# First attention of an eight-layer kernel: the mixture's largest weights loaded in sixteen pieces, and the next sequence's normalization moved half a pair of heads forward

## The chip, the cores and the metric

The kernel runs on one core of a Trainium2 chip. A core has TensorE (PE: matrix products; its weight loads, PEld, are shown apart), VectorE (DVE), ScalarE (ACT), GpSimd (POOL) and SyncE (SP), which only starts DMAs here. Each engine works through its own queue in order; semaphores let one engine wait for another or for a DMA. The metric is the device time of one launch in microseconds (us), as the median of several runs; less is better.

## The reference, cut to what matters

The reference is a chain of eight layers over `x` of 4 sequences x 1024 tokens x 128 channels: attention, mixture of experts, gated attention, the mixture again, a state space layer, a gated feed-forward layer, a second attention, and the feed-forward layer again. The change touches the first attention and the weights of the mixture:

```python
x = x + attention(layernorm(x))     # 16 heads of 64, causal
x = x + mixture(layernorm(x))       # 8 experts, 2 per token

def attention(x):                   # per sequence and head
    q, k, v = x @ Wq, x @ Wk, x @ Wv
    s = where(causal, -big, (q / 8) @ k.T)
    return softmax(s) @ v -> all heads @ Wo + bo

# mixture: W1 (8, 128, 512) and W2 (8, 512, 128), 2 MB each
h = relu(buf[e] @ W1[e] + b1[e]);  y = h @ W2[e] + b2[e]
```

## The kernel before, in words

The layers follow each other. `x` stays in SBUF throughout. The constructors of all layers load their weights first, on SP's queue, the first attention's own (Wq, Wk, Wv, Wo) on ACT's queue. Two loads are deferred: `load_late` (L91) puts the load of W1 and that of W2 (2 MB each, L496 and L497) as closures into a list `k.late`, ahead of which the state space layer has put a small exp on ACT (L1033, result `a`), with its DVE partner in `k.late_v` (L1034). The mixture needs W1 and W2 only after the first attention is over.

**First attention.** It works on 32 pairs of heads n, eight for each of the four sequences. For a pair, the queries are taken in four units (n, gq), gq = 0 to 3, of two blocks of 128 rows each; block i sees the first i + 1 blocks of keys. `first_stages` and `probabilities` make the scores (PE, L352), take them out of PSUM with the mask and the running minimum of their negatives (DVE, L358, a custom instruction that writes `p` and `tops`), and take the exponential with the sum (ACT, L367). At the end of a unit DVE forms the reciprocal `r` of the sums (L380), SP writes it to DRAM (`shares`, L383, 512 elements of 4 bytes) and reads it back spread over the partitions (`share`, L386). This first stage runs ahead of the second by up to 20 blocks of scores (`ahead`, `LEAD`).

`outputs` is the second stage: for each step PE transposes two columns of blocks of `p` into PSUM tiles `t` (L426), one is copied to `pt` by DVE (L433) and one by ACT (L431), and one step later PE multiplies `pt` with the values into `o` (L451). At the end of a unit DVE multiplies `o` by `share` into `ot` (L458). PSUM gives `s` two buffers, `t` two, `o` one, and the other products one (`ps_m`).

Between the steps one element of a list `pieces` is run at a time: projections of the pair after next (L280, L291), the output product of the pair before (`joined`, L318, L322), and, once in a sequence, the transposes of the normalized next sequence. `normalized(b)` (L248) computes the layer norm of sequence b into `xl`: eight statistics and eight aggregations on DVE (L117, L119), a square root on ACT (L121, which has to load another function table than the exponential and later load the old one back), a reciprocal (L122) and eight scalings (L124) on DVE; then POOL adds the bias `bo` to `x` (L251); then it appends two pieces that transpose `xl` to `xt` (L260). It is called ahead of unit (n, 0) when n + 2 is the first pair of a sequence, so for n = 6, 14 and 22.

**What sets the order.** `k.order()` gives chains (`pe`, `ve`) that keep PE's and part of DVE's instructions in the order in which the program writes them; the rest is placed by a scheduler, which also places the semaphore waits. DMAs started by hardware queues take turns on eight semaphore lanes: a DMA waits on its issuing engine until the DMA that had its lane before has landed.

The deferred loads are released in `probabilities`: at the first unit with gq = 2, after the exp of its first block (block 4), the whole list is run at once, pinned behind that exp in ACT's queue.

Of the kernel before, what the change touches and what calls it, by code (L numbers as in the profile page):

```python
# [21 lines left out]
B = 4  # L22
# [39 lines left out]
class Kernel:  # L62
# [28 lines left out]
    def load_late(self, pool, name, shape, src):  # L91

        t = pool.tile(shape, F32, name="w_" + name)
        self.late.append(lambda: self.nc.scalar.dma_start(t, src))
        return t

    def broadcast_row(self, pool, name, width):
# [97 lines left out]
class AttentionA:  # L195
# [11 lines left out]
    Q = 2  # L207
    NQ = NC // 2
# [12 lines left out]
    def __call__(self, start=None):  # L221
        k, tc, nc = self.k, self.k.tc, self.k.nc
        wq, wk, wv, wo, bo = self.wq, self.wk, self.wv, self.wo, self.bo
        Q, NQ, NP = self.Q, self.NQ, HEADS // 2
        scale = 1.0 / math.sqrt(DH_A)
        with self.stack as ctx:
# [15 lines left out]
                out=mask[:, MW - P :], in_=mask[:, MW - P :], compare_op=ALU.is_ge, fill=MASKED, base=0,  # L242
                pattern=[[-1, P]], channel_multiplier=1,
            )
            xts, pairs, units = {}, {}, {}
            pieces = []

            def normalized(b):  # L248
                xl = one.tile([P, NC, C], F32, tag="xl", name="xl")
                k.normalize(xl, k.xb(b), pin=ve)  # L250
                nc.gpsimd.tensor_tensor(  # L251
                    k.xb(b), k.xb(b), bo.unsqueeze(1).to_broadcast([P, NC, C]), ALU.add
                )

                def turned(h):
                    if h == 0:
                        xts[b] = one.tile([P, T], F32, tag="xt", name="xt")
                    ps = ps_m.tile([P, 512], F32, tag="m", name="ps")
                    for c in range(4):
                        pe(nc.tensor.transpose(ps[:, c * P : (c + 1) * P], xl[:, h * 4 + c, :], k.ident))  # L260
                    k.evacuate(xts[b][:, h * 512 : (h + 1) * 512], ps)

                pieces.extend([(NP * b, lambda: turned(0)), (NP * b, lambda: turned(1))])

            def projected(n):

                b, g = divmod(n, NP)
                cols = slice(g * P, (g + 1) * P)
                qt = sb.tile([P, T], F32, tag="qt", name="qt")
                kt = sb.tile([P, T], F32, tag="kt", name="kt")  # L270
                if g % 2 == 0:
                    both = sb.tile([P, NC, 2 * P], F32, tag="vv", name="vv")
                    for m in range(2):
                        pairs[n + m] = dict(v=both[:, :, m * P : (m + 1) * P])
                pairs[n].update(q=qt, k=kt)

                def features(to, w, h):
                    half = slice(h * 512, (h + 1) * 512)
                    ps = ps_m.tile([P, 512], F32, tag="m", name="ps")
                    pe(nc.tensor.matmul(ps, w[:, cols], xts[b][:, half], start=True, stop=True))  # L280
                    if w is wq:
                        nc.scalar.mul(to[:, half], ps, scale)
                    else:
                        nc.vector.tensor_copy(to[:, half], ps)

                def values(h):

                    ps = ps_m.tile([P, 2, 2 * P], F32, tag="m", name="ps")
                    for c in range(2):
                        j = h * 2 + c  # L290
                        pe(nc.tensor.matmul(  # L291
                            ps[:, c, :], xts[b][:, j * P : (j + 1) * P], wv[:, g * P : (g + 2) * P],
                            start=True, stop=True,
                        ))
                    k.evacuate(both[:, h * 2 : h * 2 + 2, :], ps)

                pieces.extend([
                    (n, lambda: features(qt, wq, 0)), (n, lambda: features(kt, wk, 0)),
                    (n, lambda: features(qt, wq, 1)), (n, lambda: features(kt, wk, 1)),
                ])  # L300
                if g % 2 == 0:
                    pieces.extend((None, lambda h=h: values(h)) for h in range(4))
# [33 lines left out]
            def probabilities(n, gq):  # L336

                q, kk = pairs[n]["q"], pairs[n]["k"]
                p = (late if gq == NQ - 1 else one).tile(
                    [P, 2, Q, (gq + 1) * Q * P], F32, tag=f"p{gq}", name="p"  # L340
                )
                tops = sb.tile([P, 2, Q, 2], F32, tag="tops", name="tops", bufs=3)
                sums = sb.tile([P, 2, Q], F32, tag="sums", name="sums")
                for i in range(Q):
                    ib = gq * Q + i
                    width = (ib + 1) * P
                    for at, lo in enumerate(range(0, width, 512)):
                        hi = min(lo + 512, width)
                        s = ps_s.tile([P, 2, 512], F32, tag="s", name="s")
                        for h in range(2):  # L350
                            feats = slice(h * DH_A, (h + 1) * DH_A)
                            pe(nc.tensor.matmul(  # L352
                                s[:, h, : hi - lo], q[feats, ib * P : (ib + 1) * P], kk[feats, lo:hi],
                                start=True, stop=True,
                            ))
                        m = mask[:, MW - hi + lo :] if hi == width else mask[:, : hi - lo]
                        for h in range(2):
                            ve(nc.vector.tensor_tensor_reduce(  # L358
                                p[:, h, i, lo:hi], s[:, h, : hi - lo], m, -1.0, 3.4e38, ALU.add, ALU.min,
                                tops[:, h, i, at : at + 1],  # L360
                            ))
                        if hi < width:
                            yield (hi - lo) // P
                    if width > 512:
                        nc.vector.tensor_tensor(tops[:, :, i, 0], tops[:, :, i, 0], tops[:, :, i, 1], ALU.min)  # L365
                    for h in range(2):
                        exp = nc.scalar.activation(  # L367
                            p[:, h, i, :width], p[:, h, i, :width], AF.Exp, bias=tops[:, h, i, 0:1],
                            scale=-1.0, accum_out=sums[:, h, i : i + 1],
                        )  # L370
                    if k.late and gq == 2:
                        pin = k.order()
                        pin(exp)
                        while k.late:
                            pin(k.late.pop(0)())
                        while k.late_v:
                            ve(k.late_v.pop(0)())
                    if i == Q - 1:
                        r = sb.tile([P, 2, Q], F32, tag="r", name="r")
                        nc.vector.reciprocal(r, sums)  # L380

                        there = dram.tile([2, Q, P], F32, tag="shares", name="shares")
                        nc.sync.dma_start(there.rearrange("h i p -> p h i"), r)  # L383
                        share = sb.tile([P, Q * P], F32, tag="share", name="share", bufs=4)
                        for h in range(2):
                            nc.sync.dma_start(  # L386
                                share[h * DH_A : (h + 1) * DH_A],
                                there[h : h + 1].rearrange("h i p -> h (i p)").to_broadcast([DH_A, Q * P]),
                            )
                        units[n, gq] = p, share  # L390
                    yield (hi - lo) // P

            def first_stages():
                for n in range(B * NP):
                    while n not in pairs or any(owner == n for owner, _ in pieces):
                        yield None
                    for gq in range(NQ):
                        yield from probabilities(n, gq)
# [48 lines left out]
            def product(n, gq, o, share, products, last, at_end):  # L447
# [7 lines left out]
                if at_end:  # L455
# [4 lines left out]
                    )  # L460

            normalized(0)
            projected(0)
            projected(1)
            ahead()
            for n in range(B * NP):
                for gq in range(NQ):
                    if gq == 0 and n + 2 < B * NP and (n + 2) % NP == 0:
                        normalized((n + 2) // NP)
                    if gq == 1 and n > 0:  # L470
                        joined(n - 1)
                    if gq == 3 and n + 2 < B * NP:
                        projected(n + 2)
                    outputs(n, gq)
# [1359 lines left out]
```

## Time and profile before

| | |
|---|---|
| median of 3 runs | 3373.56 us (3370.95 to 3374.28) |
| the profiled execution, its own time | 3378.53 us |
| its span, first to last instruction | 3376.7 us |
| mean granted clock of PE | 0.947 of full speed |
| first attention, from the first transpose to the last product into `ot` | 9.7 to 1220.6 us |
| bytes moved by DMAs, whole span | 109.35 MB |
| ACT's load of W1, issued | 34.8 us, 0.38 us long |
| ACT's load of W2, issued | 50.3 us, 0.88 us long |
| square root of the normalization, four times in the stage | 0.30 us each |
| scalings of the normalization (L124), 128x128 | 0.34 us each |
| last product into `ot` of pairs 0 to 6 ends at | 106.4, 142.8, 177.1, 213.5, 247.9, 290.0, 326.2 us |

A row of the profile names the line of the program, the engine, the operation and the tiles (written <- read). In the order of time a row has the start and the length in us; in brackets stands how long the engine was idle before it and what ended that. A row of windows has, for each engine, the busy time and the number of instructions in that stretch, then the clock that PE was granted, the mean busy share of the DMA engines, and GB/s. A duration of PE is to be read with the clock: at 0.5 the same product takes twice as long.

### The profile page before, as it was taken

The page shows a single profiled execution, that of the slowest core. Times are in us where ns is not written, and L with a number is a line of the kernel's source. Part 1 is how long each engine was busy: PE and PEld are TensorE (multiplying, and loading weights), DVE is VectorE, ACT ScalarE, POOL GpSimd, SP SyncE. Part 2 cuts the span into 40 slices and gives each one's busy share as a digit, 9 for nine tenths or more (in the row PEclk, how much of TensorE's full clock was granted, in tenths as well). Part 3 has the DMA queues.
Part 4 walks back from the last instruction along what each step waited for, and adds up shares of the span by engine and source line. Part 5 has one row for each costly group of instructions (what it writes and reads, how often), then busy time and mean ns, then how long its engine had stood idle before and what let it go on. Part 6 is the DMA issues. An engine that isn't in the chain of part 4 may idle for free.

```text
span 3376.7 us, 45533 instructions
## 1 busy us (share of the span) xinstructions
PE 3015.2 (89%) x16624; PEld 1655.0 (49%) x16624; DVE 2306.0 (68%) x5281; ACT 1812.9 (54%) x3819; POOL 273.0 (8%) x269
## 2 busy tenths in 40 slices
PE   5999999999999979869988597978778799999988
PEld 2555555555455547635566344444445344444435
DVE  3666666666776656666566589897977677677634
ACT  2555555555555523445423597979654265556662
POOL 1000000000000002530013200000001101010000
PEclk8999999999999989989999798989999699899999
DMA  5110111111110101100001111111111112121100
GB/s 156 16 16 14 15 18 16 14 17 17 14 17 15 15 8 32 53 10 1 0 16 40 53 64 50 57 57 51 63 38 42 34 44 53 31 51 31 30 2 25
DMA packets 149537, 109.35 MB, mean 32 GB/s; under 512 B 91760, under 2 KB 130432, under 8 KB 146880
## 3 DMA queue, kind: packets, MB, share of 16 engines
q1 hardware_dynamic: 128352, 72.84, 9.4%
q0 software_dynamic: 17408, 27.32, 3.3%
q10 hardware_dynamic: 3552, 6.29, 0.6%
q8 instruction: 130, 2.13, 0.4%
q14 instruction: 95, 0.78, 0.1%
HBM read 90.76 MB, written 15.60 MB: 31 GB/s over the span
## 4 chain that ended last, share of the span: by engine, by line
PE 68%; DVE 11%; ACT 8%; DMA 6%; issue 6%; POOL 1%; SPq 0%; DVEq 0%; ACTq 0%; POOLq 0%
PE s L352 8%; PE t L426 8%; PE o L451 8%; PE acc L649 4%; PE o L1613 4%; PE acc L1227 4%; PE x L1579 3%; PE ps L280 3%; PE acc L948 3%; PE s L1515 3%; ACT p L1585 3%; DMA shares<-r 2%; ACT hc L1226 2%; DVE st L1214 2%; DVE tops L1524 2%
## 5 line engine op out<-in xcount | busy, mean ns | idle before, releaser
L358 DVE CUSTOM_DVE_ANT_0 p<-s,mask 128x512 f32<-128x512 f32 (+3 forms) x768 | 394.6, 553 | 170.5 <-PE s L352 168.3
L367 ACT ACTIVATE p<-p,tops 128x640 f32<-128x640 f32 (+7 forms) x512 | 391.7, 767 | 146.1 <-DVE tops L365 85.4
L1585 ACT ACTIVATE p<-x 128x512 f32<-128x512 f32 (+3 forms) x768 | 337.6, 490 | 246.4 <-PE x L1584 176.6
L1524 DVE TENSOR_REDUCE tops<-s 128x2 f32<-128x1024 f32 (+3 forms) x384 | 361.3, 956 | 133.8 <-PE s L1520 94.2
L431 ACT COPY pt<-t 128x512 f32<-128x512 f32 (+1 forms) x320 | 157.7, 493 | 380.0 <-PE t L426 379.5
L1227 PE MATMUL acc<-hc,ident 128*128 128x512 f32 x512 | 270.1, 652 | 93.2 <-ACT hc L1226 92.3
L352 PE MATMUL s<-kt,qt 64*128 64x512 f32 (+3 forms) x1536 | 339.4, 533 | 2.7 <-DVE tops L358 2.6
L451 PE MATMUL o<-pt,vv 128*64 128x256 f32 (+1 forms) x2560 | 323.3, 374 | 14.7 <-ACT pt L431 9.4
L426 PE MATMUL t<-ident,p 128*128 128x128 f32 x2304 | 326.2, 282 | 3.7 <-DVE pt L433 3.0
L426 PEld LDWEIGHTS t<-ident,p 128*128 128x128 f32 x2304 | 248.1, 142 | 103.3 <-issue 70.0
L1214 DVE TENSOR_TENSOR_SCAN st<-decay,st 128x1024 f32<-128x1024 f32 x128 | 288.8, 2279 | 10.9 <-ACT decay L1211 10.4
L451 PEld LDWEIGHTS o<-pt,vv 128*64 128x64 f32 x2560 | 156.6, 137 | 263.9 <-issue 157.3
L433 DVE COPY pt<-t 128x512 f32<-128x512 f32 x320 | 220.0, 687 | 66.0 <-PE t L426 66.0
L1579 PE MATMUL x<-q,k 75*128 75x512 bf16 (+3 forms) x768 | 223.1, 338 | 27.7 <-ACT p L1585 15.0
L1515 PE MATMUL s<-k,q 72*128 72x512 bf16 (+3 forms) x768 | 216.3, 348 | 31.9 <-DVE tops L1524 17.6
L1226 ACT ACTIVATE hc<-ps,by_time 128x256 f32<-128x256 f32 x512 | 200.7, 478 | 50.6 <-PE ps L1220 50.5
L352 PEld LDWEIGHTS s<-kt,qt 64*128 64x128 f32 x1536 | 112.5, 188 | 180.7 <-issue 139.7
L1227 PEld LDWEIGHTS acc<-hc,ident 128*128 128x128 f32 x512 | 91.7, 198 | 209.6 <-ACT hc L1226 191.0
L738 POOL DMA_INDIRECT got<-y_rows,rows x128 | 136.7, 1068 | 645.1 <-DMA y_rows<-y 543.5
L1213 DVE TENSOR_TENSOR st<-du,bs 128x1024 f32<-128x1024 f32 x128 | 151.8, 1217 | 49.4 <-PE ps L1220 49.2
L649 PE MATMUL acc<-d,xl 128*128 128x480 f32 (+1 forms) x384 | 152.8, 559 | 26.2 <-DVE d L644 26.2
L1220 PEld LDWEIGHTS ps<-ident,st 128*128 128x128 f32 x1024 | 126.0, 146 | 96.5 <-issue 60.7
(272 smaller groups left out, 4740.7 us busy)
## 6 DMA issues: line engine op xcount, KB each, us to landing
bs<-b_rows SPq DMA_DIRECT2D x64, 512.0 KB
share<-shares SPq DMA_DIRECT2D x256, 64.0 KB
k<-b_parts POOLq DMA_DIRECT2D x16, 576.0 KB, 13.2
q<-b_parts POOLq DMA_DIRECT2D x48, 192.0 KB, 12.1
b_parts<-part SPq DMA_DIRECT2D x24, 256.0 KB
y_rows<-y SPq DMA_DIRECT2D x16, 192.0 KB
x<-in_x_dram SPq DMA_DIRECT2D x4, 512.0 KB
w_W<-in_W_dram ACTq DMA_DIRECT2D x1, 2048.0 KB
```

The lines of the kernel that those rows point to most:

```text
L352: pe(nc.tensor.matmul(s[:, h, : hi - lo], q[feats, ib * P : (ib + 1) * P], kk[feats, lo:hi], start=True, stop=True,))
L358: ve(nc.vector.tensor_tensor_reduce(p[:, h, i, lo:hi], s[:, h, : hi - lo], m, -1.0, 3.4e38, ALU.add, ALU.min, tops[:, h, i, at : at + 1],))
L367: exp = nc.scalar.activation(p[:, h, i, :width], p[:, h, i, :width], AF.Exp, bias=tops[:, h, i, 0:1], scale=-1.0, accum_out=sums[:, h, i : ...
L426: pe(nc.tensor.transpose(t[:, h, i * P : (i + 1) * P], p[:, h, i, jb * P : (jb + 1) * P], k.ident))
L451: pe(nc.tensor.matmul(o[feats, lo:], pairs[n]["v"][:, jb, feats], pt[:, h, lo:], start=jb == 0, stop=jb == last,))
L649: pe(nc.tensor.matmul(acc[n][:, :m, :].rearrange("p e s -> p (e s)"), xl[:, c, :], d[:, e : e + m, :].rearrange("p e s -> p (e s)"), start ...
L1214: nc.vector.tensor_tensor_scan(st, decay, st, 0.0, ALU.mult, ALU.add)
L1227: nc.tensor.matmul(acc[:, c : c + 2, :].rearrange("p c d -> p (c d)"), k.ident, hc.rearrange("p c d -> p (c d)"), start=n == 0, stop=n == ...
L1515: start.pin(nc.tensor.matmul(s[:, a, : hi - lo], qq[:ROWS, two + a, ib * P : (ib + 1) * P], kk[:ROWS, two + a, lo:hi], start=True, stop=ha ...
L1524: nc.vector.tensor_reduce(tops[:, half, two : two + 2, n], s[:, :, : hi - lo], AX.X, ALU.max)
L1579: start.pin(nc.tensor.matmul(x[:, lo:], kk[:FULL, a, jb * P : (jb + 1) * P], qq[:FULL, a, hq * 512 + lo : (hq + 1) * 512], start=True, sto ...
L1585: nc.scalar.activation(p[:, a, lo:], x[:, lo:], AF.Exp)
```

## The change

Two edits. The deferred loads become sixteen DMAs of 256 KB, one per expert and matrix; one element of the list is run at the end of a unit (after the exps of its second block), from unit (0, 2) on, so the small exp `a` in (0, 2) and the pieces in (0, 3) to (4, 2). And `normalized(b)` is cut in two: its arithmetic (DVE, ACT, POOL) runs ahead of unit (n, 2) with n + 3 the first pair of a sequence (n = 5, 13, 21); the rest, now `across(b)`, which only appends the two pieces of transposes, stays ahead of unit (n, 0) with n + 2 the first pair (n = 6, 14, 22). The scheduler leaves PE's order as it was. Around the third place it also moves statistics of the mixture's first two normalizations, and sets four table loads there in place of two.

```diff
@@ load_late
         t = pool.tile(shape, F32, name="w_" + name)
-        self.late.append(lambda: self.nc.scalar.dma_start(t, src))
+        self.late.extend(
+            lambda at=at: self.nc.scalar.dma_start(t[:, at], src[:, at]) for at in range(shape[1])
+        )
         return t
@@ AttentionA.__call__
-            xts, pairs, units = {}, {}, {}
+            xls, xts, pairs, units = [], {}, {}, {}
...
             def normalized(b):
                 xl = one.tile([P, NC, C], F32, tag="xl", name="xl")
                 k.normalize(xl, k.xb(b), pin=ve)
                 nc.gpsimd.tensor_tensor(
                     k.xb(b), k.xb(b), bo.unsqueeze(1).to_broadcast([P, NC, C]), ALU.add
                 )
+                xls.append(xl)
+
+            def across(b):
+                xl = xls.pop()
 
                 def turned(h):
...
-                    if k.late and gq == 2:
+                    if k.late and i == Q - 1 and n * NQ + gq > 1:
                         pin = k.order()
                         pin(exp)
-                        while k.late:
-                            pin(k.late.pop(0)())
+                        pin(k.late.pop(0)())
                         while k.late_v:
                             ve(k.late_v.pop(0)())
...
             normalized(0)
+            across(0)
             projected(0)
             projected(1)
             ahead()
             for n in range(B * NP):
                 for gq in range(NQ):
+                    if gq == 2 and n + 3 < B * NP and (n + 3) % NP == 0:
+                        normalized((n + 3) // NP)
                     if gq == 0 and n + 2 < B * NP and (n + 2) % NP == 0:
-                        normalized((n + 2) // NP)
+                        across((n + 2) // NP)
```

## The prediction, made before the changed kernel was run

> **What bounds the kernel now.** I read the page first (busy shares, then the chain), then the stage windows of the first attention (0 to about 1222 us, the only stage that the diff touches), then the order of time at the two places that the diff touches. An engine's busy share says little here, so the question at each place is only: does TensorE (PE) stop, and for what.
>
> ```profile
> PE 3015.2 (89%) x16624; PEld 1655.0 (49%) x16624; DVE 2306.0 (68%) x5281; ACT 1812.9 (54%) x3819; POOL 273.0 (8%) x269
> ...
> PE 68%; DVE 11%; ACT 8%; DMA 6%; issue 6%; POOL 1%; SPq 0%; DVEq 0%; ACTq 0%; POOLq 0%
> ```
>
> PE carries the chain. The stage windows (busy time and count per engine, granted clock, share and rate of DMA) show where it does not run:
>
> ```profile
> core 0: us, PE busy (x) PEld busy (x) DVE busy (x) ACT busy (x) POOL busy (x), PEclk, DMA share, GB/s
> 26.00:36.50 10.50, 8.39 (x42) 3.76 (x40) 8.23 (x35) 5.99 (x19) 2.53 (x3) 1.00 0.57 168
> 36.50:44.00 7.50, 4.53 (x17) 2.47 (x16) 2.34 (x6) 0.00 (x0) 1.02 (x1) 0.77 0.99 280
> 44.00:58.00 14.00, 4.58 (x20) 2.94 (x18) 0.95 (x6) 5.51 (x13) 0.00 (x0) 0.63 0.30 84
> 58.00:71.00 13.00, 9.60 (x44) 5.50 (x42) 5.85 (x15) 2.18 (x4) 0.00 (x0) 0.74 0.42 103
> 71.00:84.20 13.20, 9.35 (x23) 3.14 (x24) 2.85 (x11) 4.90 (x14) 0.00 (x0) 0.61 0.02 1
> 84.20:106.40 22.20, 22.20 (x139) 11.96 (x139) 14.99 (x45) 10.34 (x24) 0.00 (x0) 1.00 0.13 13
> 106.40:142.80 36.40, 36.40 (x227) 19.74 (x226) 24.57 (x77) 19.57 (x46) 0.00 (x0) 1.00 0.10 16
> ```
>
> From 84.2 on PE is busy all the time at full clock: a pair of heads takes 34.4 or 36.35 us and no other engine matters. Before, in 36.5 to 84.2, PE works at a clock of 0.61 to 0.77 with holes. What makes the holes (start, length, what; in brackets the idle time before it and its end):
>
> ```profile
> 50.28 0.02 ACT L94 MOVE_SHAPE w_W<-in_W_dram  x1 [17.23 <-DMA w_b<-in_b_dram]
> 50.34 0.88 ACTq L94 DMA_DIRECT2D w_W<-in_W_dram  x1
> 50.51 3.53 SPq L386 DMA_DIRECT2D share<-shares  x4
> ...
> 53.52 0.70 PE L451 MATMUL o<-pt,vv 128*64 128x128 f32 x4 [9.42 <-ACT pt L431]
> ```
>
> The second big load (W2) sits in ACT's queue and waits for the landing of b2's load, whose semaphore lane it inherits. b2 lies behind W1's 2 MB, so ACT stands for 17.2 us and PE, which needs ACT's copy pt, for 9.4 us. Then the shares' loads (64 KB) crawl beside W2: issued at 50.5, used by DVE at 60.9.
>
> The other place is the change of sequence, three times (pair 6, 14, 22):
>
> ```profile
> 282.80 1.28 ACT L121 ACT_TABLE_LOAD   x1
> ...
> 284.10 0.30 ACT L121 ACTIVATE rstd<-mv,eps 128x8 f32<-128x8 f32 x1
> 284.43 0.20 DVE L122 RECIPROCAL rstd<-rstd 128x8 f32<-128x8 f32 x1 [1.32 <-ACT rstd L121]
> ...
> 284.67 2.14 DVE L124 TENSOR_SCALAR xl<-x,mv,rstd 128x128 f32<-128x128 f32 x8
> ...
> 285.07 1.24 PE L260 MATMUL ps<-ident,xl 128*128 128x128 f32 x4 [3.79 <-DVE xl L124]
> ```
>
> PE waits 3.79 us for the first normalized block, and its next four transposes take 1.24 us where the next group of four takes 0.60.
>
> **Part 1: the loads.** Removed: two issues of 2 MB behind the exp of block 4. Added: after the exps of unit (0,2) only the small exp `a`; then one piece of 256 KB after each of the units (0,3) to (4,2). The changed program's order shows PE's order untouched and ACT's free of the block: after the exp of block 5 come copies as they fall due. What is late next? By its list of waits DVE now has the reciprocal r of unit (0,2) ahead of the scores of block 6, and that r reuses a buffer which the write of unit (0,0)'s shares to DRAM must have left. So DVE stands for that landing, and the product into ot stands for the shares read back.
>
> When does it land? SP issues the write at 36.1 as before. In the steady part a write of 512 elements of 4 B needs 5.6 to 11.2 us until SP goes on with the load behind it, mostly 8.4 (73.09 to 83.43, 85.56 to 93.66). The Trainium skill, DMA: Bandwidth & Descriptors, section Anatomy of one DMA, puts a small transfer's fixed cost at about 2.0 us, most of it the write receipt (of the other descriptor path; here it is only an estimate). By that it lands at 38.7; by the row at 44 to 46.5. I take the row: 45.5.
> From there, by hand: r (0.17) and block 6's four score evictions (two of 512 columns, 1.30 with their reads, two of 384, 1.03) lead DVE to 48.0; the share's load, issued at 45.6 and 2.4 us long (83.43 to 85.9), is there at 48.0 too; ot starts at about 48.4. Before it started at 60.9. Saved: 12.5 us. Behind it the chain is the same as before (ot, copies, exp of block 7, projections of pair 1, clock half for part of it), so the 12.5 stay. PE still has a hole, 41 to 47. Bounds: landing at 38.7 saves 12.5 + 6.8, about 19 to 21; landing as late as before (50.4) still saves the slow share load, about 8.
>
> The sixteen issues: near rows are SP's 0.37 to 0.60 and ACT's own 0.38 and 0.88; I take 0.5 each, 8 us of ACT in pairs where it is half idle. Queued behind a piece is a copy pt (or, after block 7's exps, the next unit's exps, then pt); PE needs that pt for its next but one transposes, 1.6 to 2.3 us later. Two pieces (units 3 and 0) fall together there: 1.0 of 1.6 us. So hidden, barely: 0 to 6 us in all (four pairs at 1.5), I take 1. Cover gone, it is 8. Each piece also waits for its lane: those of a unit (n,1) for the piece issued at (n-1,3), 8.4 us earlier by the exps of before (262.0 to 270.4). I expect that landed or nearly so.
>
> **Part 2: the normalization.** Removed at each change of sequence: the hole and what follows. Pairs 5 and 6 take 42.16 + 36.20 us where an ordinary two take 36.35 + 34.37; about 1.0 of it is the eight extra transposes, which stay. That makes 6.6, 6.8 and 7.35 us (pairs 21 and 22: 43.39 + 35.68), together 20.8. Moved to unit (5,2): 16 statistics instructions, sqrt between two table loads, reciprocal, eight 128x128 scalings, and the 2.35 us addition on POOL, which had been idle for 249 us there; no DMA. Around 254 us of before, PE is full and DVE has gaps of 1.7 us at most. By the changed order: scores end at 254.6; statistics to 256.2, aggregates to 256.9, copy pt to 257.5; the table load stands without a wait behind vv (256.8 to 258.0), sqrt to 258.35; reciprocal 258.6; ot, then eight scalings (2.14) to 261.1; only then the scores that were ready at 257.2, to 262.4. PE meets it at 260.1: the second tile of block 1's scores needs that score buffer and waits 2.3 us. After that copies and buffers come in time again.
>
> The clock: the skill, TensorE: Matmul & The Clock Gate, section HAM oscillation, says holes up to about 3.4 us do not cool the array; by that 2.3 us costs 2.3. This trace is stricter:
>
> ```profile
> 70.80:73.40 2.60, 0.02 (x1) 0.02 (x1) 0.18 (x1) 2.53 (x5) 0.00 (x0) 1.00 0.01 3
> 73.40:76.80 3.40, 2.62 (x3) 0.78 (x4) 0.69 (x1) 0.00 (x0) 0.00 (x0) 0.57 0.07 1
> 1202.30:1203.80 1.50, 0.07 (x2) 0.07 (x4) 0.55 (x3) 0.60 (x2) 0.00 (x0) 1.00 0.00 0
> 1203.80:1207.20 3.40, 3.40 (x28) 2.18 (x29) 1.41 (x3) 2.61 (x5) 0.00 (x0) 1.00 0.47 5
> ```
>
> A hole of 2.6 us halves the clock afterwards, one of 1.5 does not. Ours lies between, so I charge 1.2 of the 2.0 us that a drop cost at 285. With 0.4 for the disturbed order after it: 3.9 us each. At the third place six statistics of the mixture's own normalization fall into the block (0.4 beyond the wait for sqrt), and its four table loads are 2.6 us more on an idle ACT: 4.3. Saved: 20.8 - 3.9 - 3.9 - 4.3 = 8.7, say 8. Bounds: 13 (no drop, nothing else), 3 (drop each time and a late copy).
>
> **Sum.** -12.5 + 1 - 8 = -19.5 us. The profiled execution took 3378.5 us (span 3376.7), the median of the runs is 3373.56; stalls of this size are not scaled, so 3373.6 - 19.5 = 3354.
>
> **Rivals.**
> - The shares land early (2 us, the skill's price): 3354 - 7.5, about 3346. For it: nothing else is on the queue then. Against: every steady row. 0.15.
> - The shares land as late as before, since b2's 1024 small elements or the two writes, not W1, made the delay: part 1 gives 8, 3359. For it: W1, b2 and the first shares all landed within 50.1 to 50.45. Against: twelve of their sixteen parts were there by 44 to 47. 0.12.
> - Moving the normalization gives nothing: DVE's 6.5 us block makes a hole as long as the old one, clock drop included. 3373.6 - 11.5 + 0, 3362. 0.08.
> - Slower: the pieces hold ACT as W2 did. If a piece lands only when the shares' writes beside it do, and they take 14.3 us as under W1 (36.1 to 50.4), ACT stands in each unit (n,1) of pairs 1 to 4 for 14.3 - 8.4 - 0.6 (cover left) and the clock drops (2.0): 4 x 7.3 = 29 us against 20.5 saved, 3382. It decides from a landing of about 12 us on. Against: 256 KB is an eighth of W1. 0.04.
>
> The likeliest case has 0.61, its own range 3346 to 3361. The range reaches to 3342 (early landing with a cheap move) and 3366 (late landing, costly move). About 0.2% (6.7 us) is what a measurement of this kernel can tell from no change. Faster by more: the likeliest and the early landing whole, 0.10 of the late one, 0.04 of the move that gives nothing, 0.90 together; within it the rest of these two, 0.06; slower 0.04.
>
> **What would show it.** Right: no ACT wait of 15 us at the loads; ot's first product near 48; a DVE wait for shares of some 8 us before 46; the hole before the transposes of xl gone, and holes of about 2.3 us before scores one pair earlier; pairs 1 to 4 still at 34.4 and 36.35. Wrong: pairs 1 to 4 longer (pieces cost), pairs 5, 13, 21 still near 42 (the move only shifts the hole), or ot's first product after 52.

## The result, and the profile after

The changed kernel takes 3396.31 us (median of 4 runs, 3395.58 to 3398.64), the kernel before beside it 3372.26 us. The ratio is 1.007, with a 95% interval of 1.0054 to 1.0087: slower by some 24 us, where 19.5 us less were forecast. The profiled execution of the changed kernel took 3395.73 us (span 3393.9), 17.2 us more than that of the kernel before, which was itself 6 us above its median. All of the 17 us arise in the first attention: its last product into `ot` ends at 1238.0 us where it ended at 1220.6, and the layers behind it are shifted by as much.

The head of the page hardly shows it. PE's share of busy time is 89% as before, and the chain that ended last adds up to 44% here: it no longer reaches back into the first attention.

```profile
PE 3027.4 (89%) x16624; PEld 1660.5 (49%) x16624; DVE 2307.3 (68%) x5281; ACT 1815.8 (54%) x3820; POOL 272.4 (8%) x269
...
PE 24%; DVE 7%; ACT 7%; issue 4%; DMA 2%; POOL 0%; DVEq 0%; ACTq 0%; POOLq 0%; SPq 0%
```

So the stage has to be cut at the ends of the pairs. Windows of the changed kernel: the start in two, the rest of pair 0, and then pairs 1, 2 and 6.

```profile
core 0: us, PE busy (x) PEld busy (x) DVE busy (x) ACT busy (x) POOL busy (x), PEclk, DMA share, GB/s
36.50:48.60 12.10, 7.58 (x42) 3.88 (x38) 3.97 (x13) 3.39 (x8) 1.17 (x1) 0.91 0.20 19
48.60:71.00 22.40, 17.74 (x64) 8.31 (x64) 8.77 (x27) 8.88 (x20) 0.00 (x0) 0.67 0.15 23
71.00:93.40 22.40, 22.40 (x141) 12.14 (x140) 15.02 (x45) 10.70 (x26) 0.00 (x0) 1.00 0.21 44
93.40:129.70 36.30, 36.30 (x227) 19.69 (x226) 24.58 (x76) 19.60 (x46) 0.00 (x0) 1.00 0.18 43
129.70:174.20 44.50, 37.87 (x216) 19.34 (x216) 24.21 (x77) 18.52 (x44) 0.00 (x0) 0.92 0.24 38
...
293.50:338.70 45.20, 37.65 (x217) 19.39 (x216) 24.26 (x76) 18.56 (x45) 0.00 (x0) 0.92 0.16 17
```

Pair 0 ends at 93.4 (106.4 before): 13.0 us are won, as forecast. Pair 1 is full. Pair 2 has as many products as before (216) but lasts 44.5 us (34.4 before); PE is idle for 6.6 us of it, and its clock is 0.92 on average. Pair 6 is of the same kind. Pair lengths, from the last product into `ot` of one pair to that of the next:

| pair | before | after | |
|---|---|---|---|
| 0 | 106.4 | 93.4 | -13.0 |
| 1, 3 | 36.3, 36.4 | 36.3, 36.3 | 0 |
| 2, 4 | 34.4, 34.4 | 44.5, 41.8 | +10.2, +7.4 |
| 5 and 6 | 42.2 + 36.2 | 41.1 + 45.3 | +8.0 |
| 13 and 14 | 42.4 + 36.1 | 40.8 + 42.4 | +4.7 |
| 21 and 22 | 43.4 + 35.7 | 42.1 + 35.0 | -2.0 |
| all others | | | +2.2 |
| all 32 | 1220.6 | 1238.0 | +17.4 |

The two places that the change was made for look as the prediction said. First the start, in the order of time of the changed kernel (in brackets the idle time before the row and what ended it):

```profile
44.63 0.18 DVE L385 RECIPROCAL r<-sums 128x4 f32<-128x4 f32 x1 [5.76 <-DMA shares<-r]
44.67 2.45 SPq L391 DMA_DIRECT2D share<-shares  x4
...
48.69 0.42 DVE L463 TENSOR_TENSOR ot<-o,share 128x256 f32<-128x256 f32 x1 [1.54 <-DMA share<-shares]
...
57.22 0.35 ACTq L95 DMA_DIRECT2D w_W<-in_W_dram  x1
```

DVE waits at `r` for the shares' write until 44.6 (forecast 45.5), the first product into `ot` starts at 48.7 (forecast 48.4), and the first piece is issued at 57.2 with no stall of ACT. Then the normalization in its new place, in pair 5:

```profile
262.61 0.30 ACT L123 ACTIVATE rstd<-mv,eps 128x8 f32<-128x8 f32 x1
262.95 0.20 DVE L124 RECIPROCAL rstd<-rstd 128x8 f32<-128x8 f32 x1 [1.14 <-ACT rstd L123]
263.39 2.13 DVE L126 TENSOR_SCALAR xl<-x,mv,rstd 128x128 f32<-128x128 f32 x8
...
266.80 0.70 PE L358 MATMUL s<-kt,qt 64*128 64x256 f32 x4 [1.96 <-DVE tops L364]
```

PE's hole is 1.96 us (forecast 2.3), at the scores, and the old hole of 3.79 us is gone. So the time was not lost at the two places that the change was made for, but behind them, in pairs 2, 4, 6 and 14.

What is late there? The queue of SP tells. Here is the kernel before, at the step from pair 1 to pair 2; L383 writes the shares of a unit to DRAM, L386 reads them back in two DMAs:

```profile
120.76 2.12 SPq L383 DMA_DIRECT2D shares<-r  x2
128.87 4.10 SPq L386 DMA_DIRECT2D share<-shares  x4
133.06 1.28 SPq L383 DMA_DIRECT2D shares<-r  x1
143.70 1.08 SPq L386 DMA_DIRECT2D share<-shares  x2
144.84 0.58 SPq L383 DMA_DIRECT2D shares<-r  x1
```

And the changed kernel at the same step (L388 writes, L391 reads):

```profile
116.68 0.59 SPq L388 DMA_DIRECT2D shares<-r  x1
126.53 1.09 SPq L391 DMA_DIRECT2D share<-shares  x2
127.67 0.58 SPq L388 DMA_DIRECT2D shares<-r  x1
138.88 1.09 SPq L391 DMA_DIRECT2D share<-shares  x2
140.01 0.59 SPq L388 DMA_DIRECT2D shares<-r  x1
```

A read waits at the head of SP's queue until its own write has landed, 8 to 11 us, and every write behind it waits too. Before, the writes of the units (1,3) and (2,0) stand side by side ("x2"): their landings overlap, and four units cost SP three waits. After, the two are apart, each read is followed by one write, and four units cost four waits: the writes of units (2,0) to (2,3) come 11 to 12 us apart (116.7, 127.7, 140.0, 151.4), where PE needs 8.6 us for a quarter of this pair. The write of (2,1) is issued 11.4 us after its `r` is done. Behind it DVE stands, in the waits for the read and for the old write:

```profile
135.66 0.42 DVE L463 TENSOR_TENSOR ot<-o,share 128x256 f32<-128x256 f32 x1 [3.18 <-DMA share<-shares]
...
160.65 0.18 DVE L385 RECIPROCAL r<-sums 128x4 f32<-128x4 f32 x1 [5.01 <-DMA shares<-r]
```

And PE stands behind DVE. These are all of PE's waits in pair 2 (what waits, for what; us in total, times, longest), together the 6.6 us:

```profile
PE t L431 <- DVE pt L438: 2.5, 1, 2.5
PE ps L286 <- DVE kt L290: 2.3, 1, 2.3
PE o L456 <- DVE ot L463: 1.8, 2, 1.2
```

SP's order of writes and reads is the same in both kernels but for four places: the two writes are apart at (1,3), (3,3), (5,3) and (13,3), and the pairs behind these, 2, 4, 6 and 14, are the ones that lose. At (21,3) they stay together, and pair 22 loses nothing.

### The profile page after: what moved, and what is told of

It is laid out like the page before. It is cut to its first block, busy times and chain, and to the rows that moved or that the text cites. A ratio compares the mean times of both kernels' runs of the same rounds, so it can differ in the third digit from the quotient of the medians.

```text
span 3393.9 us, 45539 instructions
## 1 busy us (share of the span) xinstructions
PE 3027.4 (89%) x16624; PEld 1660.5 (49%) x16624; DVE 2307.3 (68%) x5281; ACT 1815.8 (54%) x3820; POOL 272.4 (8%) x269
## 6 DMA issues: line engine op xcount, KB each, us to landing
k<-b_parts POOLq DMA_DIRECT2D x16, 576.0 KB, 12.5
q<-b_parts POOLq DMA_DIRECT2D x48, 192.0 KB, 11.6
```

## Experiments

Theory S: the loss is this chain on SP, write, landing, read, next write. Rivals: P, the sixteen pieces slow the other transfers or hold ACT; M, the normalization's new place costs more than its hole; later also D, DVE held at `r`, and Q, F as the expectations say. The kernel before took between 3374.94 and 3396.94 us in the four groups of runs, which were made on two chips; so each run is given as its ratio to the kernel before of its own group, and the parts are measured by the lengths of the pairs. Pairs that wait for nothing have the same length in every trace (pair 11: 36.3 to 36.4 us wherever SP issues the reads). Those that wait do not: in two profiled executions of the changed kernel itself the first attention took 1238.0 and 1258.8 us, and pairs 1 to 4 together 159.0 and 166.3. A difference of a few us in such pairs proves little by itself.

**Order alone, taken away and put back.** Both kernels below hold back a unit's reads in the program until the next unit's write has been written down, and pin SP's order; the other engines' orders are unchanged.

```diff
-nc.sync.dma_start(there..., r)
+sp(nc.sync.dma_start(there..., r))          # sp = k.order()
+held.append((share, there))
+if not (hold(n, gq)):                       # which units' reads go behind the next write
+    while held: ... sp(read), sp(read)
```

The kernel before, with the reads ahead of the next write at those four places only:

> The kernel before with one thing changed: at the four changes of pair where the changed kernel has lost the doubled write on SP's queue (units (1,3), (3,3), (5,3), (13,3)) the two reads of the shares are queued ahead of the next unit's write, not behind it. All other orders are those of the kernel before. Theory S (SP's queue order is the loss): pairs 2, 4, 6 and 14 grow as in the changed kernel, by 10, 7, 9 and 6 us, so about +33 us, 3405 (from +25 on I count it as shown). Rival P (the sixteen pieces cost the time: their transfers slow the shares' small writes, or their issues hold ACT): no piece is here, so within 3 us of the kernel before, 3372.

Measured: ratio 1.0054 (1.0039 to 1.0069), +18 us (3393.05 against 3374.94). Pairs 2, 4 and 6 took 45.1, 44.5 and 39.6 us (+10.7, +10.1, +3.4), and pair 14 lost nothing; the stage is 23.6 us longer. No piece and no moved normalization is in this kernel: order alone makes most of the loss. It stays short of the 25 us from which the expectation would count S as shown, at pairs 6 and 14, and the reason can be read: with the normalization in its old place those pairs begin with PE's hole, and the reads of units (6,0) to (6,2) land 13 to 15 us ahead of `ot` in the kernel before, against 4 to 10 in pair 2. The old hole was slack for SP.

The changed kernel, with the writes side by side again:

> The changed kernel with one thing put back: at those four changes of pair the next unit's write stands ahead of the reads on SP's queue, as in the kernel before. PE's, DVE's, ACT's and POOL's orders are those of the changed kernel. Theory S: the 33 us go, 3396 - 33 = 3363, and the 13 us of pair 0 show, so 9 us faster than the kernel before, perhaps up to 16. Rival P: the order does not matter, 3390 to 3396, pairs 2 and 4 still 42 to 44 us. Rival M (the normalization's new place costs): pairs 6 and 14 stay at 42 to 45 and only pairs 2 and 4 recover, 3379.

Measured: ratio 0.9978 (0.9968 to 0.9987), 3368.81 us. The first attention shrinks from 1238.0 to 1214.2 us. Pairs 2, 4, 6, 14 take 37.6, 35.7, 41.6, 35.0. So the order was worth about 24 us in the stage (about 31 by the two ratios), and the change turns from a loss into a small gain; yet pairs 2 and 6 stay 3.2 and 5.4 us too long, so the order is not all. In pair 2 a read landed late: that of (2,2) was issued at 143.0 and landed at 155.5, 0.1 us before `ot` used it. In pair 6 the writes of (6,1) and (6,2) still went out 6.0 and 5.6 us after their `r`.

**Each half of the change alone.**

> The kernel before with the loads in 16 pieces and the normalization where it was. SP's order has the single writes at (1,3) and (3,3) and the doubled ones elsewhere. Theory S: pair 0 gains 13, pairs 2 and 4 lose 10 and 7, 3372 + 4 = 3376, all other pairs as before. Rival P: the same losses or, if the pieces cost in every pair they fall into, pairs 1 to 4 each longer; rival M: 3372 - 13 = 3359.

Measured: ratio 1.003 (1.0017 to 1.0043), some 10 us where S said 4. Pair 0 93.9; pairs 1 to 4 38.0, 46.7, 39.0 and 43.2, together 25.4 us longer than before. The order alone (first experiment) made 21.0 of that. The other 4 would be a small part for rival P, but they are less than the 7.3 us by which the changed kernel differs from itself in these pairs, so they are not shown.

> The kernel before with the normalization one pair earlier and the loads as they were. SP's order has the single writes at (5,3) and (13,3) and the doubled one at (21,3). Theory S: pairs 6 and 14 lose 9 and 6, pairs 5, 13 and 21/22 give back 1 to 2 each, about +11, 3383; pairs 21 and 22 together about 2 shorter than before. Rival P: no pieces, so the recorded gain of 8, 3364. Rival M: pairs 21 and 22 lose as well, some 7 us at each of the three places, 3393.

Measured: ratio 1.0032 (1.0017 to 1.0047), +12 us; pairs 6 and 14 44.6 and 46.7, pairs 21 and 22 together 2.9 shorter than before. No piece is in this kernel, so P can't explain it; and where the writes stay side by side the move gains, so M can't either. A move of DVE's work loses 12 us by what it does to SP's queue. That the old hole was slack shows here too: with the same order at (13,3), pair 14 lost nothing with the hole (first experiment) and 10.6 us without.

**The reads taken off SP's queue.** If SP is only a queue, another queue for the reads should cure it. POOL issues them (`nc.gpsimd.dma_start` for `nc.sync.dma_start`); from unit (0,2) on all writes then go out within 0.03 us of their `r`.

> The changed kernel with the two reads of the shares issued by POOL, so that SP's queue holds the writes alone and no write waits behind a read. PE's, DVE's and ACT's orders are unchanged. Theory S (on SP each read holds the next unit's write until its own write has landed): all four losses go and also what was left of them with the doubled writes (pairs 2, 4, 6: 3.2, 1.4, 5.4 us), so the gain forecast at first appears, about 3355 (up to 3360). Rival P (pieces) or rival M (the move): pairs 2 and 4, or 6 and 14, stay 3 us or more above the kernel before; 3369 or more. Rival Q: POOL issues more slowly, or its own queue now holds the reads; then the spare time between a read's landing and ot goes to zero in every pair and the time is above 3396.

> The kernel before with the reads issued by POOL, the control for the last. There the write is already early enough (the read landed 2 us or more ahead of ot nearly everywhere), so theory S gives nothing: 3370 to 3375. If POOL's reads help by themselves, whatever the order, as much as in the changed kernel, it is below 3360.

> The kernel before with the loads in 16 pieces only, reads issued by POOL. Theory S: pair 0 shorter by 12 to 13 and pairs 1 to 4 as before: 3373 - 12.5 = 3361. Rival P (pieces slow the small writes or hold ACT): pairs 1 to 4 longer by 1 us or more each, 3365 and above.

> The kernel before with the normalization one pair earlier only, reads issued by POOL. Theory S: the gain of 8 that the prediction gave this part, from pairs 5 and 6, 13 and 14, 21 and 22 together: 3365. By what pairs 21 and 22 showed in the changed kernel (2.0 us shorter) it would be 6: 3367. Rival M: no gain, 3373.

Measured: ratios 1.0054 (1.004 to 1.0068), 1.0096 (1.0082 to 1.011), 1.0058 (1.004 to 1.0077), 1.0087 (1.0072 to 1.0103): all slower than the kernel before. Against each other they are what the prediction said of the parts: the loads -13.1 us (3405.48 against 3418.58), the move -5.0 (within the intervals), both -17.0. But S as a matter of SP's queue alone falls: the writes are on time and `ot` still waits. Rival Q has the nearest number (3401.59), but not for its reason: an issue takes POOL 0.5 us. The kernel before with POOL's reads, at the step to pair 3:

```profile
173.45 2.22 POOL L386 DMA_DIRECT2D share<-shares  x4 [13.50 <-DVE r L380]
184.65 1.03 POOL L386 DMA_DIRECT2D share<-shares  x2 [8.97 <-DMA shares<-r]
187.99 0.42 DVE L458 TENSOR_TENSOR ot<-o,share 128x256 f32<-128x256 f32 x1 [3.21 <-DMA share<-shares]
```

The product at 187.99 needs the first pair of these reads, issued from 173.5 to 174.0. They landed at 187.9 only, 14 us later. In that time two small writes were on their way, (3,0) until 174.1 and (3,1) from 173.2 to 184.1. Over the stage, a read landed more than 6 us after its issue in 15% of the units of the kernel before (median 3.6 us), and in 71 to 73% (median 9.3 to 9.8) with the reads on POOL.

Is POOL's path slower by itself? The trace of the kernel before with POOL's reads tells it apart. In pairs 1 to 31, 169 of its reads were issued while the write of another unit was on its way: all of them landed after that write, in a median of 11.6 us. The 66 reads that had no such write on its way, nor one within 2.5 us behind them, took 2.5 to 3.9 us, no longer than SP's. So POOL's path is not slow by itself; its reads are late where a small write is under way. The Trainium skill, DMA: Bandwidth & Descriptors, section Queues, rings and completion order, has a rule that fits: the semaphore increment of a transfer lands only after every earlier write of that DMA engine, across its queues. It is stated there for the queues of SP and ACT; the trace agrees with the sequence (the reads issued at 173.5 landed after the write that ended at 184.1) and doesn't show the cause. It is not the whole either: in the kernel before, 22 of the 23 reads on SP's queue that took over 6 us had the next write issued within 2.5 us behind them, not ahead of them. So the theory is sharpened: a small write blocks not only SP's queue, but also delays the reads near it on any queue. The write itself has to become cheap.

**The write made cheap.** The shares are laid out as head, position, block, so that a unit's write is 256 pieces of 8 B, not 512 of 4 B; `ot` reads `share` with a stride. Orders unchanged, the four places with the writes apart included.

```diff
-there = dram.tile([2, Q, P], ...)   # written "h i p -> p h i"
+there = dram.tile([2, P, Q], ...)   # written "h p i -> p h i"
```

> The changed kernel with the shares laid out in DRAM by head, position, block (not head, block, position), so that the write of a unit is 256 pieces of 8 B where it was 512 of 4 B; ot reads the share with a stride of 8 B. No engine's order changes, SP's single writes at (1,3), (3,3), (5,3), (13,3) stay. Theory S, sharpened by the last runs (the small write holds the rings for 8 to 11 us, and both the next write and the reads stand behind it): a landing of about 5 us instead of 9, the chain write, read, read at 6 to 7 us a unit, below the 8.6 to 9.1 that PE needs, so pairs 2, 4, 6 and 14 at their lengths of before and the forecast gain shows, 3353 to 3358. Rival F (the landing is a fixed receipt, not a cost of each piece): landing stays 8 to 9, pairs 2, 4, 6 and 14 stay at 42 to 45, 3396. Rival P or M: pairs 2 and 4, or 6 and 14, longer in spite of a landing of 5 us.

> The kernel before with the same layout of the shares, the control. Theory S: the shares' landing at the start is still behind W1 and ACT's stall stays, and no pair waits for shares later, so 3370 to 3374, at most 4 us less. If it falls to 3360 or less, the gain of the last run is the layout's and not the change's.

Measured on one chip: 3356.82 us (ratio 0.9886, 0.9867 to 0.9904) against 3377.95 us (0.9944, 0.9927 to 0.996). With cheap writes the change is worth 21.1 us. That this is near the 19.5 of the prediction is in part luck: the first attention gains 15.1 us, of which pair 0 gives 7.3, pairs 1 to 4 take back 0.9, and the normalization gives 8.7. Landing falls from 9.0 us to 3.3 on average over pairs 1 to 31, no read takes over 6 us, and SP, with the writes side by side or apart, has time left. SP's queue around the step to pair 3 in the changed kernel with this layout:

```profile
138.44 2.01 SPq L388 DMA_DIRECT2D shares<-r  x2
141.16 2.86 SPq L391 DMA_DIRECT2D share<-shares  x4
146.17 0.37 SPq L388 DMA_DIRECT2D shares<-r  x1
149.49 1.08 SPq L391 DMA_DIRECT2D share<-shares  x2
```

The write at 146.17 is followed by its read 3.3 us later, and 9 us pass until the next write (158.4): SP waits for DVE; DVE waits for no share after pair 0. Pairs 2, 4, 6, 14: 35.3, 34.4, 35.0, 35.0. F falls. The expectation for the control was too small: the kernel before gains 19 us of its own, by a start 10.4 us shorter (pair 0 at 96.0) and by shorter last pairs (28, 30 and 31 together 8.7); those waits had been there before the change. So of the 40 us between the changed kernel with this layout and the kernel before, the layout has 19 and the change 21. Of the 21.1, 6 lie outside the first attention; between profiled executions on one chip the rest of the program varies by up to 22 us (2143 to 2165), so these 6 are left open.

**DVE's wait at `r`.** Six buffers for `r` where there were two:

> The changed kernel with six buffers for the reciprocals r where there are two, so that DVE never waits at r for an old write to leave (55 us of waits in the changed kernel); all orders unchanged. Theory S (SP's chain is what is late, the wait at r is only its first sign): the write is still late, ot still waits for the share, pairs 2, 4, 6 and 14 stay above 40, 3385 to 3396. Rival D (DVE held at r is the loss, through the scores behind it): these pairs go back to their lengths of before, 3360 to 3366.

Measured: ratio 1.0016 (1.0006 to 1.0026), 3403.39 us beside 3396.94. Pairs 2, 4 and 6 still take 41.8, 46.6 and 43.4 us: without the wait at `r`, DVE stands for the shares instead, 58.6 us in 17 places of the first attention where it was 23.8 in 8. There D falls as the cause. But pair 14 is back at 36.9 us, against S, and pair 0 is 4 us shorter than in the changed kernel; by the ratios (1.0016 beside 1.007, of different groups of runs) some 18 of the 24 us are gone. So both waits are ways in which the late write costs time, and how much of the loss goes through each is left open.

**The halves again with cheap writes, the changed kernel on the same chip, and what makes a write slow.** In the last kernel each reciprocal is written twice side by side, so the write keeps its 512 pieces, but of 8 B.

> The kernel before with the loads in 16 pieces only, shares written in 256 pieces of 8 B. Theory S (the two parts are worth what they look like once SP's chain has slack): pair 0 at 88.7 as in the changed kernel with this layout, 7.4 under the 96.0 of the kernel before with this layout; pairs 1 to 4 within 1 us of it; 7 to 8 us below that kernel's time. Rival P (the pieces cost): pairs 1 to 4 together 3 us or more longer, and so 4 us below at most.

> The kernel before with the normalization one pair earlier only, shares written in 256 pieces of 8 B. Theory S: pairs 5 and 6, 13 and 14, 21 and 22 shorter than those of the kernel before with this layout by 1.9, 3.4 and 3.4 us, together 8.7 (forecast 8). Rival M: 3 us or less.

> The changed kernel itself, beside the two with the new layout and on the same chip, so that the loss can be stated there. Theory S: pairs 2, 4, 6 and 14 again above those of the kernel before, by 25 to 35 us together, and slower than the kernel before by 10 to 25 us; the two runs with the new layout have no loss in these pairs.

> The changed kernel with each reciprocal written twice side by side, so that a unit's write is 512 pieces of 8 B where the changed kernel has 512 of 4 B (and the two reads 128 KB where they were 64 KB; ot takes every other element). It tells what the 8 B did. If the number of pieces sets the landing: 9 us as with 512 of 4 B, the losses stay, 3390 or more. If pieces of 4 B are the slow ones: landing 4 to 5.5 us, pairs 2, 4, 6 and 14 at their lengths of before, 3356 to 3364.

Measured: ratios 0.989 (0.9862 to 0.9917), 0.9866 (0.9838 to 0.9894), 1.0101 (1.0074 to 1.0127) and 0.9861 (0.9834 to 0.9888). Loads alone: pair 0 at 87.2, 8.8 us below the control's 96.0, which was taken on the other chip, and 11.6 below that of the move alone (98.8), whose loads are as before; pairs 1 to 4 together 0.9 longer. Move alone: the three places 3.5, 3.4 and 3.1 us shorter, together 9.9. The changed kernel loses again, in the same pairs (45.1, 45.2, 46.2, 46.3, together 41.7 us more than before where 25 to 35 were expected). With 512 pieces of 8 B the landing is 4.05 us and no pair loses: it is the size of 4 B that is slow, not the number. This kernel, 3336.02 us beside 3384.89, beats both kernels.

## Why the prediction was wrong

- **The loads, 12.5 us.** Right to the place: landing 44.6 (said 45.5), `ot` at 48.7 (said 48.4), pair 0 13.0 shorter. ACT does not stall at the pieces. With cheap writes it is 7.3 to 11.6 us.
- **"Behind it the chain is the same as before ... so the 12.5 stay."** This is the step that failed, with its twin in part 2, "After that copies and buffers come in time again". They were read off PE's, DVE's and ACT's orders; SP's was not looked at, since no DMA of the shares was added or removed. But the scheduler put the reads of a pair's last unit ahead of the next write at four places: (1,3) and (3,3) by the loads alone, (5,3) and (13,3) by the move alone, as the orders of these two kernels show (why it does so is not shown). That cost about 24 us in the stage (1238.0 against 1214.2, order put back), more by the ratios.
- **The sum that was missing.** The prediction had used the rows itself: a write that takes 5.6 to 11.2 us, mostly 8.4, until SP goes on (by the semaphores 7.3 to 11.2, median 8.7, in pairs 1 to 31). Four of them in a row with their issues (1.1 for two reads, 0.6 for the write) are 40 us, more than the 34.4 and 36.35 of a pair. Before the change SP was already close to being the bound (from 120.8 to 154.5 it issues or stands for landings, 33.7 of the 35.4 us until 156.2, where the next two writes go out), and only the overlap of two landings per pair kept it below. SP's own list of waits said so in the kernel before, 723.6 of the 1100 us from 100 to 1200 spent on writes that had not landed:

```profile
SPq L386 <- DMA shares<-r: 723.6, 111, 10.6
```

  And DVE's wait at `r` for an old write to leave was there too, 36.8 us in 20 places.
- **The pieces, +1 us.** 0.9 with cheap writes, as said. With the slow ones it may be 4 to 5 (the loads alone against the order alone: 4.4; pairs 1 to 4 with the order put back: 5.0), which is within what two executions of one kernel differ by in these pairs.
- **The normalization, 8 us.** Hole 1.96 (said 2.3). It gains 9.9 us alone where the writes are cheap, 8.7 with the loads beside it. With the old writes it lost 12 us alone, in pairs 6 and 14, where the old hole no longer hides SP's chain.
- **The clock.** 1.2 of 2.0 us was charged per hole as undecided. In the changed kernel each of the three holes of 1.96 us was followed by 3.41 us at a clock of 0.5, so 3.4 us is not what it takes. But with cheap writes one such hole of three was, and with the move alone and cheap writes none of three (1.96, 1.96 and 2.31 us). The granted clock changes only at the ends of windows of 3.41 us (last section), so these are the rows to look at. First the hole from 264.84 on of the changed kernel, then that from 252.72 on of the move alone, which lies across the end of a window:

```profile
264.95:268.36 3.41, 1.56 (x12) 0.79 (x12) 3.41 (x10) 0.93 (x2) 2.35 (x1) 1.00 0.02 7
268.36:271.77 3.41, 3.41 (x12) 1.79 (x10) 1.97 (x11) 3.41 (x11) 0.00 (x0) 0.50 0.00 0
...
249.94:253.35 3.41, 2.78 (x22) 1.58 (x18) 2.53 (x11) 2.64 (x4) 0.00 (x0) 1.00 0.00 0
253.35:256.76 3.41, 2.08 (x16) 1.22 (x17) 3.41 (x11) 0.93 (x2) 2.35 (x1) 1.00 0.00 0
256.76:260.17 3.41, 3.41 (x22) 1.58 (x20) 3.16 (x13) 3.41 (x13) 0.00 (x0) 1.00 0.05 3
```

  In the first, PE is idle for 1.85 us of one window; in the second, for 0.63 and 1.33 us of two. So both readings of the prediction looked at the length of a hole alone, and its place counts as well; a charge of 1.2, between the two, came near by luck.
- **The slower rival** (pieces hold ACT as W2 did, 3382) named the wrong engine: ACT waited for no piece. Its kind of mechanism, a queue that stands until a small write has landed, was right, one queue further.

## What to carry to other kernels

Add up, for every queue that only issues transfers, what one round of the loop costs it including the landings that it stands for, and compare with the round of the bounding engine; here a queue that was taken up to 95% had no busy share on the page at all, and lost at the first shift. When a change moves instructions under a scheduler, compare the order of every queue, also of those whose instructions it doesn't touch. And where single 4-byte elements are written to DRAM on the way to something that waits, try another layout early: pieces of 8 B took the kernel before down by 19 us, and the changed kernel, on one chip, from 3416.51 to 3336.02 us.

## What the runs showed of the hardware

- A write of 512 pieces of 4 B from SBUF to DRAM landed after 9.0 us on average (changed kernel, pairs 1 to 31), 512 of 8 B after 4.05, 256 of 8 B after 3.3 (its two variants). Doubling the size of each piece at the same number halves the time. Why 4 B is slow isn't shown; 256 pieces of 4 B weren't tried.
- A read near such a write lands late: with the reads on POOL, all 169 that were issued while another unit's write was on its way landed after it (median 11.6 us, the one at 174.0 after 14 us), where the 66 with no write near took 2.5 to 3.9 us. On SP's queue 22 of 139 reads with a write issued within 2.5 us behind them took over 6 us, and none of the 55 with no write near. A read of 64 KB takes 2.4 us at best.
- PE's clock changes on a grid: in all 17 traces every stretch of one clock lasts a multiple of 3.41 us. Between 80 and 1215 us they have 5495 such windows at full clock. All 86 in which PE, by the busy time that the traces give, was idle for 1.85 us or more were followed by one at 0.5, and none in which it was idle for less than 1.7 us; between these both occur. So a hole of 1.96 us halves the clock if nearly all of it lies in one window, and doesn't if it is split between two. In the kernel with cheap writes the one drop of three cost about 1.5 us (pairs 5 and 6 gained 1.9, the two other places 3.4 each).
